# A second split level for the second MLP product of a DiT block, with inner weight sets made in the first half

## The chip, the cores and the metric

The kernel runs on one core of a Trainium2 chip. The metric is the device time of one execution in microseconds. All data is fp32. The engines of a core are TensorE (PE, with its weight loads as PEld), VectorE (DVE), ScalarE (ACT), GpSimd (POOL) and SyncE (SP), which only issues transfers.

## The reference

One DiT block on x of 2 x 2048 tokens with 576 channels: adaptive layer norm, attention with 16 heads, a projection with gated residual, a second adaptive layer norm and an MLP of width 2304 with a gated residual. The part that the change touches is the MLP:

```python
x = x + g_msa[:, None, :] * o
xn2 = _ln(x, 1e-06)
xn2 = xn2 * (1 + sc_mlp[:, None, :]) + sh_mlp[:, None, :]
h = jax.nn.gelu(xn2 @ w1 + b1, approximate=False)   # 576 -> 2304
m = h @ w2 + b2                                     # 2304 -> 576
x = x + g_mlp[:, None, :] * m
```

## The kernel before

Tokens are worked in 8 blocks (NB) of 512 (BLK). P is 128, PAIR 256, C 576, HALF 288. The width of 2304 is 18 groups (NF) of 128, of which HF = 9 make a half, and MH is 1152. Everything ahead of the MLP's two products is untouched, but for how w1 is brought in.

**The first half** makes gelu(xn2 @ w1 + b1) in 72 jobs, 9 for each token block. A job is one product of 512 tokens with 2 x 128 columns of w1, split once in the manner of Strassen and Winograd: seven products of 256 x 256 pieces in place of eight. `whole_part` is 28 matmul instructions of 256 columns (L1977), `last_part` 8 more in single-pass f32r for the last 64 rows (L1991). The weights and their sums lie in `wb` (seven sets). Two PSUM tiles, the sides, are used in turn, so a side is written again two jobs later. Then `gelu_stored`: ACT copies one product out of PSUM (L2003), DVE combines the seven in four operations that read PSUM (L2004 to L2011), ACT applies gelu to two 128x512 pieces (L2015) and SP stores each to `gelus` in DRAM (L2016, 256 KB). The four results lie in a ring of two `cs` tiles.

Between the jobs `ahead` prepares the next block's tokens, tile by tile of 128, one tile for two jobs: POOL loads a tile (L1026), DVE makes its statistics and normalizes it (L277, L279, L283, L288; ACT gives the root, L281, with a table load), DVE transposes 32x32 squares (L1042), POOL stores them to DRAM in four pieces, `turned` (L1047), and loads them back turned, whole chunks into `xnt` (L1055) and the last 64 rows twice into `parts` (L1057); ACT modulates both (L1064, L393, L394), POOL forms a difference (L395). `token_sums` adds the block's outer token sums on DVE.

**The second half** multiplies with w2 and adds the residual: 16 groups q of 256 tokens, each again split once, seven products of 128 tokens x 1152 x 288, nine matmuls of 288 columns each, which the program issues as two instructions: 2016 of L2137. Four weight quarters and three sums lie in `ws`, made in the first half. The token sums `as` are five DVE operations of 128x1152 for each q (L2115); DVE combines and applies gate and residual (L2141 to L2174), POOL adds the gated bias to the residual rows (L2120) and issues the output (L2175). `hidden` is loaded by SP, three slots of 2.3 MB. The first two products of a group use `hidden` as it is.

**What sets the order.** DVE's order is the one in which the code is written (`manual_schedule`). For PE, ACT, POOL and SP the scheduler places instructions, each engine then works its list strictly in order. A DMA stands in the queue of the engine that issues it and waits there.

The lines:

Of the kernel before, what the change touches and what calls it, by code (L numbers as in the profile page):

```python
# [8 lines left out]
F32 = mybir.dt.float32  # L9
# [22 lines left out]
def dit_block(  # L32
# [724 lines left out]
    def block_of_small():  # L757
# [1111 lines left out]
        gelus = [dram.tile([NPART, P, NF, PAIR], F32, name=f"gelu{n}") for n in range(NB)]  # L1869
# [11 lines left out]
        wb = mw.tile([P, 7, 2, MH], F32, name="wb")  # L1881
# [4 lines left out]
        for i, (k, f) in enumerate(((0, 0), (0, 1), (1, 0), (1, 1))):  # L1886
            nc.scalar.dma_start(
                out=wb[:, i],
                in_=w1[k * PAIR : (k + 1) * PAIR, f * MH : (f + 1) * MH].rearrange("(k p) f -> p k f", p=P),
            )  # L1890
        nc.scalar.dma_start(out=last_rows, in_=w1[512:576, :].rearrange("p (a f) -> p a f", a=2))
        for j in range(TPB + 1):
# [10 lines left out]
            lambda: nc.vector.tensor_tensor(wb[:, 4], wb[:, 1], wb[:, 0], ALU.subtract),  # L1903
            lambda: nc.vector.tensor_tensor(wb[:, 1], wb[:, 3], wb[:, 1], ALU.subtract),
            lambda: nc.vector.tensor_tensor(wb[:, 5], wb[:, 3], wb[:, 4], ALU.subtract),
            lambda: nc.vector.tensor_tensor(wb[:, 6], wb[:, 5], wb[:, 2], ALU.subtract),
# [23 lines left out]

        close_xs = token_tiles(3)
        m2, close_m2 = opened("m2", side="right")
        ws = {m: m2.tile([P, HF, HALF], F32, name=f"ws{m}") for m in (2, 5, 3, 4, 6, 7)}
        hidden = [m2.tile([P, NF, PAIR], F32, name="hidden0")]
# [3 lines left out]
        css = [m1.tile([P, 5, PAIR], F32, name=f"cs{i}") for i in range(2)]  # L1938
# [20 lines left out]
        def whole_part(n, f, side):  # L1959
# [15 lines left out]
            for m in (2, 4, 1, 5, 6, 7, 3) if n == f == 0 else (2, 4, 5, 6, 7, 3, 1):  # L1975
                for k in range(2):
                    nc.tensor.matmul(  # L1977
                        out_m[m],
                        wb[:, slot[m], k, f * P : (f + 1) * P],
                        moving[m](k),  # L1980
                        start=k == 0 and m in (1, 2, 5, 6),
                        stop=k == 1 and m == 1,
                    )
# [15 lines left out]
        def gelu_stored(n, f, side):  # L1999
            cs = css[side]  # L2000
# [11 lines left out]
            for i in range(2):  # L2012
                part = cs[:, 2 * i : 2 * i + 2, :]
                g = i * HF + f
                nc.scalar.activation(part, part, AF.Gelu, bias=b1_sb[:, g : g + 1])  # L2015
                nc.sync.dma_start(out=gelus[n][:, :, g, :].rearrange("t p c -> p t c"), in_=part)  # L2016
# [25 lines left out]
        quarters = [(2, 0, 0), (5, 1, 1), (3, 0, 1), (4, 1, 0)]  # L2042

        def quarter_loaded():
            m, k, n = quarters.pop(0)
            quarter = w2[k * HF * P : (k + 1) * HF * P, n * HALF : (n + 1) * HALF]
            nc.sync.dma_start(out=ws[m], in_=quarter.rearrange("(f p) c -> p f c", p=P))

        later_sums = [
            lambda: nc.vector.tensor_tensor(ws[6], ws[2], ws[3], ALU.add),  # L2050
            lambda: nc.vector.tensor_tensor(ws[3], ws[3], ws[5], ALU.subtract),
            lambda: nc.vector.tensor_tensor(ws[7], ws[4], ws[5], ALU.add),
            lambda: nc.vector.tensor_tensor(ws[4], ws[4], ws[2], ALU.subtract),
        ]

        def hidden_loaded(q):
            n, g = divmod(q, NPART)
            nc.sync.dma_start(out=hidden[q % len(hidden)], in_=gelus[n][g])
# [6 lines left out]
        for job in range(0, NB * HF, 2):  # L2065
# [13 lines left out]
            if job % 4 == 2 and job > 2 * HF and later_sums:  # L2079
                later_sums.pop(0)()  # L2080
            if job % 4 == 2 and quarters:
                quarter_loaded()
            if job == 4 * HF:
                hidden_loaded(0)
        stack.close()
        for close in (close_m1, close_mw, close_mx):
            close()

        close_psum = opened_psum(s=4)
        hs, close_hs = opened("hs")  # L2090
        hidden += [hs.tile([P, NF, PAIR], F32, name=f"hidden{i}") for i in (1, 2)]
        for q in (1, 2):
            hidden_loaded(q)
        ws[1] = hs.tile([P, HF, HALF], F32, name="ws1")

        def second_product(q, gate, gate_bias):

            b, t0 = divmod(q * PAIR, N)
            ht = hidden[q % len(hidden)]

            def part(t, k):
                return ht[:, k * HF : (k + 1) * HF, t * P : (t + 1) * P]

            stationary = {3: part(0, 0), 4: part(1, 1)}
            for m, x_, y_, op in (
                (2, part(1, 0), part(1, 1), ALU.add),
                (5, part(0, 0), part(0, 1), ALU.add),
                (6, part(1, 0), part(0, 0), ALU.subtract),
                (7, part(0, 1), part(1, 1), ALU.subtract),
                (1, part(0, 0), part(1, 1), ALU.add),  # L2110
            ):
                if q == 0 and m == 1:
                    nc.vector.tensor_tensor(ws[1], ws[2], ws[5], ALU.add)
                stationary[m] = hs.tile([P, HF, P], F32, name=f"as{m}")
                nc.vector.tensor_tensor(stationary[m], x_, y_, op)  # L2115
            xr = []
            for t in range(2):
                xr.append(hs.tile([P, C], F32, name="xr", bufs=2))
                nc.sync.dma_start(out=xr[t], in_=x1_dram[b, t0 + t * P : t0 + (t + 1) * P, :])
                nc.gpsimd.tensor_tensor(xr[t], xr[t], gate_bias, ALU.add)  # L2120
            last = q == NB * NPART - 1
            y = [hs.tile([P, 2, HALF], F32, name="y", bufs=3) for _ in range(2)]
            c00, c01, c10, c11 = y[0][:, 0, :], y[0][:, 1, :], y[1][:, 0, :], y[1][:, 1, :]
            ms = {}

            def half(ap, n):
                return ap[:, n * HALF : (n + 1) * HALF]

            def half_stored(t, n):
                nc.sync.dma_start(out=half(out[b, t0 + t * P : t0 + (t + 1) * P, :], n), in_=y[t][:, n, :])  # L2130

            for pair in ((3, 4), (2, 5), (6, 7), (1,)):
                ps = s_tile()
                for a, m in enumerate(pair):
                    ms[m] = ps[:, a, :HALF]
                    for f in range(HF):
                        nc.tensor.matmul(  # L2137
                            ms[m], stationary[m][:, f, :], ws[m][:, f, :], start=(f == 0), stop=(f == HF - 1)
                        )
                if pair == (3, 4):  # L2140
                    nc.vector.tensor_copy(c01, ms[3])  # L2141
                    nc.vector.tensor_copy(c10, ms[4])
                elif pair == (2, 5):
                    nc.vector.tensor_tensor(c00, c10, ms[5], ALU.subtract)
                    nc.vector.tensor_tensor(c11, c01, ms[2], ALU.subtract)
                    nc.vector.tensor_tensor(c10, c10, ms[2], ALU.add)
                    nc.vector.tensor_tensor(c01, c01, ms[5], ALU.add)
                elif pair == (6, 7):
                    nc.vector.tensor_tensor(c11, c11, ms[6], ALU.add)
                    nc.vector.tensor_tensor(c00, c00, ms[7], ALU.add)  # L2150

                if last and len(pair) == 2 and pair != (3, 4):
                    for t in range(2):
                        n = 1 - t if pair == (2, 5) else t
                        part = y[t][:, n, :]
                        nc.vector.tensor_tensor(part, part, half(gate, n), ALU.mult)
                        nc.vector.tensor_tensor(part, part, half(xr[t], n), ALU.add)
                        if pair == (2, 5):
                            half_stored(t, n)
            if last:  # L2160
                for t in range(2):
                    product = half(xr[t], t)
                    nc.vector.tensor_tensor(product, ms[1], half(gate, t), ALU.mult)  # L2163
                    nc.vector.tensor_tensor(y[t][:, t, :], y[t][:, t, :], product, ALU.add)  # L2164
                    half_stored(t, t)
                return
            if q + 3 < NB * NPART:
                hidden_loaded(q + 3)
            nc.vector.tensor_tensor(c00, ms[1], c00, ALU.add)
            nc.vector.tensor_tensor(c11, ms[1], c11, ALU.add)  # L2170
            for t in range(2):
                rows = y[t].rearrange("p a f -> p (a f)")
# [11 lines left out]
        for close in (close_psum, close_hs, close_m2, close_xs):  # L2184
            close()
# [39 lines left out]
```

## Time and profile before

| | |
|---|---|
| median of 3 executions | 3128.21 us (3128.03 to 3128.23) |
| the profiled execution | 3129.05 us, span 3127.3 us |
| first half, 72 jobs | one job is 7.00 us |
| second half | from 2631.70 us, 488.89 us on PE |
| granted TensorE clock | 1.00 |
| matmul instructions in the second half | 2016 |

How to read it: times in the trace are counted from the span's start. A group's row gives line, engine, operation, output<-input and shapes, the count, then busy microseconds and mean nanoseconds of one, then the idle time of the engine ahead of it and what ended that. A pipelined matmul's mean is its latency and not the distance to the next. A row of a DMA group ends with the median time from issue to landing. A row of windows gives a stretch and for PE, PEld, DVE, ACT and POOL the busy share with the count of instructions, then the granted clock, the DMA engines' busy share and GB/s. A row of one line gives the least, median and greatest duration.

### The profile page before, as it was taken

The page shows a single profiled execution, that of the slowest core. Times are in us where ns is not written, and L with a number is a line of the kernel's source. Part 1 is how long each engine was busy: PE and PEld are TensorE (multiplying, and loading weights), DVE is VectorE, ACT ScalarE, POOL GpSimd, SP SyncE. Part 2 cuts the span into 40 slices and gives each one's busy share as a digit, 9 for nine tenths or more (in the row PEclk, how much of TensorE's full clock was granted, in tenths as well). Part 3 has the DMA queues.
Part 4 walks back from the last instruction along what each step waited for, and adds up shares of the span by engine and source line. Part 5 has one row for each costly group of instructions (what it writes and reads, how often), then busy time and mean ns, then how long its engine had stood idle before and what let it go on. Part 6 is the DMA issues. An engine that isn't in the chain of part 4 may idle for free. (4 is left out here: it accounts for less than half of the span.)

```text
span 3127.3 us, 47006 instructions
## 1 busy us (share of the span) xinstructions
PE 3100.6 (99%) x17511; PEld 1849.1 (59%) x17511; DVE 1568.5 (50%) x2287; ACT 1477.3 (47%) x2853; POOL 712.6 (23%) x1005
## 2 busy tenths in 40 slices
PE   8999999999999999999999999999999999999999
PEld 5883333333333788533333333368888888777777
DVE  6773444444443556444444444355565554545454
ACT  2336666766667033466666666624565541000000
POOL 4650100132321355200011111013333320112111
PEclk9999999999999999999999999999999999999999
DMA  5773332233332654411122221146554434333331
GB/s 147 189 144 85 101 92 58 68 95 98 92 107 60 211 112 78 88 44 44 36 61 79 80 65 60 54 168 195 160 141 133 125 110 165 106 121 126 109 106 39
DMA packets 294838, 324.65 MB, mean 104 GB/s; under 512 B 168904, under 2 KB 225160, under 8 KB 292488
## 3 DMA queue, kind: packets, MB, share of 16 engines
q1 hardware_dynamic: 246464, 198.32, 21.9%
q0 software_dynamic: 46960, 117.92, 14.5%
q10 hardware_dynamic: 1176, 5.31, 0.5%
q8 instruction: 141, 2.31, 0.3%
q14 instruction: 97, 0.79, 0.1%
HBM read 200.50 MB, written 110.43 MB: 99 GB/s over the span
## 5 line engine op out<-in xcount | busy, mean ns | idle before, releaser
L1540 ACT ACTIVATE pt<-b 128x512 f32<-128x512 f32 x2048 | 1057.4, 608 | 482.0 <-PE b L1549 267.6
L1549 PE MATMUL b<-pt,vt 128*64 128x512 f32 x4096 | 935.0, 598 | 1.8 <-ACT pt L1540 1.8
L1549 PEld LDWEIGHTS b<-pt,vt 128*64 128x64 f32 x4096 | 271.8, 136 | 583.9 <-issue 437.7
L1536 PE MATMUL b<-qm,km 32*128 32x512 f32 x4096 | 563.8, 613 | 0.0
L1601 DVE TENSOR_TENSOR ot<-b,ot 128x512 f32<-128x512 f32 x192 | 132.8, 692 | 588.7 <-PE b L1549 588.7
L1536 PE MATMUL b<-qe,ke 16*128 16x512 f32 x2048 | 420.1, 791 | 0.0
L2137 PE MATMUL s<-ws,as 128*128 128x288 f32 x1440 | 351.8, 406 | 0.0
L1536 PEld LDWEIGHTS b<-qm,km 32*128 32x128 f32 x4096 | 190.6, 184 | 271.2 <-ACT pt L1540 211.1
L2137 PEld LDWEIGHTS s<-ws,as 128*128 128x128 f32 x1440 | 273.6, 190 | 75.6
L1143 PE MATMUL s<-wq,xnt 128*128 128x288 f32 x864 | 226.9, 406 | 2.5 <-ACT xnt L400 2.1
L1568 DVE RECIPROCAL den<-den 128x512 f32<-128x512 f32 x64 | 213.6, 3337 | 11.8 <-DMA den<-den_dram 11.8
L1977 PE MATMUL m<-xnt,wb 128*128 128x256 f32 x864 | 210.6, 379 | 2.6 <-DVE cs L2011 1.6
L1977 PE MATMUL m<-s,wb 128*128 128x256 f32 x864 | 210.0, 379 | 0.0
L1599 DVE COPY ot<-b 128x512 f32<-128x512 f32 x64 | 44.3, 692 | 273.3 <-PE b L1549 273.3
L1143 PEld LDWEIGHTS s<-wq,xnt 128*128 128x128 f32 x864 | 157.9, 190 | 38.3 <-ACT xnt L400 1.6
L1977 PEld LDWEIGHTS m<-s,wb 128*128 128x128 f32 x864 | 164.2, 190 | 22.3
L1536 PEld LDWEIGHTS b<-qe,ke 16*128 16x128 f32 x2048 | 106.7, 184 | 114.0 <-issue 113.3
L1977 PEld LDWEIGHTS m<-xnt,wb 128*128 128x128 f32 x864 | 158.8, 190 | 22.8 <-DVE cs L2011 2.5
L1047 POOL DMA_DIRECT2D turned<-squares x160 | 107.8, 681 | 197.6 <-DVE squares L1042 189.5
L2015 ACT ACTIVATE cs<-cs,b_sb 128x512 f32<-128x512 f32 x144 | 98.9, 719 | 113.0 <-DVE cs L2010 89.3
L1064 ACT ACTIVATE xnt<-xnt,mod 128x128 f32<-128x128 f32 x244 | 100.4, 481 | 98.4 <-DMA weight_sums<-sums_kept 51.3
L2137 PE MATMUL s<-ws,hidden 128*128 128x288 f32 x576 | 142.3, 406 | 0.0
(257 smaller groups left out, 3273.3 us busy)
## 6 DMA issues: line engine op xcount, KB each, us to landing
gelu<-cs SPq DMA_DIRECT2D x144, 256.0 KB
hidden<-gelu SPq DMA_DIRECT2D x16, 2304.0 KB
spare<-in_x_dram POOLq DMA_DIRECT2D x64, 288.0 KB, 3.1
x_dram<-spare POOLq DMA_DIRECT2D x64, 288.0 KB, 2.5
qm<-qk SPq DMA_DIRECT2D x256, 64.0 KB
den<-den_dram SPq DMA_DIRECT2D x128, 128.0 KB
xnt<-turned POOLq DMA_DIRECT2D x56, 256.0 KB, 4.0
turned<-squares POOLq DMA_DIRECT2D x160, 72.0 KB, 2.6
```

What stands on the lines that cost most here:

```text
L1047: queue.dma_start(out=by_square[g], in_=squares[g * SQ : (g + 1) * SQ, :].rearrange("p (k j) -> p k j", j=SQ))
L1064: nc.scalar.activation(part, part, AF.Identity, **affine(which, k, b))
L1143: nc.tensor.matmul(out_a, full[:, k, :], wq[:, k, f], start=k == 0, stop=False)
L1536: nc.tensor.matmul(ps, k[r, keys], q[r, :], start=first, stop=not first)
L1540: nc.scalar.activation(pt[:, h, :], banks[2 * c + h], AF.Exp, scale=SCALE)
L1549: nc.tensor.matmul(acc[64 * h : 64 * h + 64, :], vt[:, v0 : v0 + 64], pt[:, h, :], start=pt is pts[0][0], stop=pt is pts[-1][0],)
L1568: nc.vector.reciprocal(den, den)
L1599: nc.vector.tensor_copy(ot, acc)
L1601: nc.vector.tensor_tensor(ot, acc, ot, ALU.add)
L1977: nc.tensor.matmul(out_m[m], wb[:, slot[m], k, f * P : (f + 1) * P], moving[m](k), start=k == 0 and m in (1, 2, 5, 6), stop=k == 1 and m == 1,
L2015: nc.scalar.activation(part, part, AF.Gelu, bias=b1_sb[:, g : g + 1])
L2137: nc.tensor.matmul(ms[m], stationary[m][:, f, :], ws[m][:, f, :], start=(f == 0), stop=(f == HF - 1))
```

## The change

The second product is split twice. A block of 512 tokens x 2304 is split into four outer quadrants of 256 x 1152, giving seven outer products m (in the order 1, 2, 6, 5, 7, 4, 3); each of them is split again into pieces of 128 tokens x 512 and 144 columns, seven inner products of four matmuls, and a tail of 128 rows of the 1152 that the split leaves over, four matmuls. In all 56 block products with 32 matmuls of 144 columns, each again two instructions.

The parts:
- The 7 x 7 weight sets, 31 x 144 columns for each outer product, are made by DVE in the first half out of w2, two steps behind each pair of jobs (`weights_made`), in place of `quarter_loaded` and `later_sums`: 37 operations. SP stores them in 31 pieces to `w_kept` and loads them back, 2.28 MB for each outer product. `wb` is laid out anew, by f first, so that its early part can take weights once a job has used it.
- The outer token sums are made in `gelu_stored` on POOL, four of 128x256 for each job; the seven are stored in one transfer of 917 KB to `operands`. `cs` has seven pieces and a ring of three.
- The inner token sums, four of 128x512 for each block product, are made on POOL for even products and on DVE for odd ones, in two buffers, one product ahead (`sums_made`).
- DVE combines a block product in five operations out of PSUM, after a copy by ACT (`combined_blocks`), then the outer ones in SBUF, 128x576. An operand of 1.18 MB is loaded for each product, three slots.

The core of the diff:

```diff
-        gelus = [dram.tile([NPART, P, NF, PAIR], F32, name=f"gelu{n}") for n in range(NB)]
+        QUARTER = HALF // 2
+        WSIZE = 31 * QUARTER
+        operands = [dram.tile([7, P, HF, PAIR], F32, name=f"operands{n}") for n in range(NB)]
...
-            nc.scalar.dma_start(
-                out=wb[:, i],
-                in_=w1[k * PAIR : (k + 1) * PAIR, f * MH : (f + 1) * MH].rearrange("(k p) f -> p k f", p=P),
-            )
+            for j in range(2):
+                rows = slice(k * PAIR + j * P, k * PAIR + (j + 1) * P)
+                nc.scalar.dma_start(
+                    out=wb[:, :, i, j, :],
+                    in_=w1[rows, f * MH : (f + 1) * MH].rearrange("p (f c) -> p f c", c=P),
+                )
...
-        css = [m1.tile([P, 5, PAIR], F32, name=f"cs{i}") for i in range(2)]
+        css = [m1.tile([P, 7, PAIR], F32, name=f"cs{i}") for i in range(3)]
...
                 nc.scalar.activation(part, part, AF.Gelu, bias=b1_sb[:, g : g + 1])
-                nc.sync.dma_start(out=gelus[n][:, :, g, :].rearrange("t p c -> p t c"), in_=part)
+            tt = nc.gpsimd.tensor_tensor
+            tt(cs[:, 5, :], cs[:, 1, :], cs[:, 3, :], ALU.add)
+            tt(cs[:, 6, :], cs[:, 5, :], cs[:, 0, :], ALU.subtract)
+            tt(cs[:, 1, :], cs[:, 0, :], cs[:, 1, :], ALU.subtract)
+            tt(cs[:, 4, :], cs[:, 2, :], cs[:, 6, :], ALU.subtract)
+            nc.sync.dma_start(out=operands[n][:, :, f, :].rearrange("i p c -> p i c"), in_=cs)
...
+            steps = [
+                load,
+                lambda: None,
+                lambda: tt(all_[:, 4], side, all_[:, 0], ALU.subtract),
...
+                lambda: tt(more[:, :, 3], y22, y12, ALU.subtract),
...
-            if job % 4 == 2 and quarters:
-                quarter_loaded()
+            for _ in range(2):
+                if job >= 2 and making_weights:
+                    making_weights.pop(0)()
...
+        def sums_made(i):
+
+            x_ = operand[i % 3]
+            a11, a12, a21, a22 = (
+                x_[:, FULL * k : FULL * (k + 1), t * P : (t + 1) * P] for t in range(2) for k in range(2)
+            )
+            sums = hs.tile([P, 4, FULL, P], F32, name="sums", bufs=2)
+            tt = (nc.vector if i % 2 else nc.gpsimd).tensor_tensor
+            tt(sums[:, 0], a21, a22, ALU.add)
+            tt(sums[:, 1], sums[:, 0], a11, ALU.subtract)
+            tt(sums[:, 2], a11, a21, ALU.subtract)
+            tt(sums[:, 3], a12, sums[:, 1], ALU.subtract)
+            return {1: a11, 2: a12, 3: sums[:, 3], 4: a22, 5: sums[:, 0], 6: sums[:, 1], 7: sums[:, 2]}
...
+            for group in ((1,), (2, 6), (5, 7), (4, 3)):
...
+                        nc.tensor.matmul(
+                            out_m[m],
+                            stationary[m][:, c, :],
+                            w[:, FULL * (m - 1) + c, :],
...
+            tt(left, outs[2, 6], both(one), ALU.add)
+            tt(right, outs[5, 7], both(left[:, 1]), ALU.add)
+            tt(left[:, 1], right[:, 1], out_m[4], ALU.subtract)
+            tt(right[:, 1], right[:, 1], out_m[5], ALU.add)
+            tt(right[:, 0], right[:, 0], out_m[3], ALU.add)
...
+            now = stationary
+            if i + 1 < len(products):
+                stationary = sums_made(i + 1)
+            out_m, outs = multiplied(i, now)
+            operand_loaded(i + 3)
```

Where instructions stand now. First POOL in the first half, at the token tiles 46 and 47 (numbers behind names are those of the program; L2022 to L2025 are the four outer sums of a job, L1055 and L1057 the loads of a tile, L1047 its stores, L1026 the load of a tile to come). Before:

```order
L1055 DMA xnt_17613<-turned_19177 128x4x128
L1057 DMA parts_17614<-turned_19177 64x128 x2
L1047 DMA turned_19268<-squares 32x18x32 x4
L395 TENSOR_TENSOR parts_17614<-tail_17615,parts_17614 128x128
L1026 DMA xt_17958<-x_dram 128x576
L1055 DMA xnt_17613<-turned_19268 128x4x128
```

And with the change, the sums of jobs 25 and 26 around the same steps:

```order
L2022 TENSOR_TENSOR cs_17978<-cs_17978 128x256
L2023 TENSOR_TENSOR cs_17978<-cs_17978 128x256
L2024 TENSOR_TENSOR cs_17978<-cs_17978 128x256
L2025 TENSOR_TENSOR cs_17978<-cs_17978 128x256
L1055 DMA xnt_17617<-turned_19188 128x4x128
L1057 DMA parts_17618<-turned_19188 64x128 x2
L1047 DMA turned_19293<-squares 32x18x32 x4
L2022 TENSOR_TENSOR cs_17979<-cs_17979 128x256
L395 TENSOR_TENSOR parts_17618<-tail_17619,parts_17618 128x128
L2023 TENSOR_TENSOR cs_17979<-cs_17979 128x256
```

The tile's loads stand behind a job's four sums, and the first of the sums, L2022, waits for that job's gelu.

ACT at the same place (L393 and L394 modulate the parts, L2008 was L2003, the copy, and L2020 was L2015, the gelu). Before:

```order
L2003 COPY cs_17975<-one 128x256
L281 ACT_TABLE_LOAD
L281 ACTIVATE std<-mv,eps_65 128x1
L1064 ACTIVATE xnt_17613<-xnt_17613,mod 128x128 x4
L393 ACTIVATE parts_17614<-parts_17614,mod 128x128
L394 ACTIVATE tail_17615<-parts_17614,mod 128x128
L2015 ACT_TABLE_LOAD
L2015 ACTIVATE cs_17975<-cs_17975,b_sb 128x512 x2
```

And with the change:

```order
L2008 COPY cs_17979<-one 128x256
L281 ACT_TABLE_LOAD
L281 ACTIVATE std<-mv,eps_65 128x1
L1064 ACTIVATE xnt_17617<-xnt_17617,mod 128x128 x4
L393 ACTIVATE parts_17618<-parts_17618,mod 128x128
L394 ACTIVATE tail_17619<-parts_17618,mod 128x128
L2020 ACT_TABLE_LOAD
L2020 ACTIVATE cs_17979<-cs_17979,b_sb 128x512 x2
```

ACT's order is the same: a tile's modulation stands between a job's copy and its gelu, and waits for the loads that POOL issues.

Last, POOL at the end of the first half (L2183 to L2186 are inner sums of the first block product; cs_17979 is that of the last job). Before, the second half begins on POOL with residual rows:

```order
L395 TENSOR_TENSOR parts_17617<-tail_17618,parts_17617 128x128
L2120 TENSOR_TENSOR xr<-xr,gate_21030 128x576 x2
L2175 DMA out_dram<-y 128x576 x2
```

With the change:

```order
L2022 TENSOR_TENSOR cs_17979<-cs_17979 128x256
L2023 TENSOR_TENSOR cs_17979<-cs_17979 128x256
L2024 TENSOR_TENSOR cs_17979<-cs_17979 128x256
L2025 TENSOR_TENSOR cs_17979<-cs_17979 128x256
L2183 TENSOR_TENSOR sums<-operand_17965 128x512
L2185 TENSOR_TENSOR sums<-operand_17965 128x512
L2184 TENSOR_TENSOR sums<-sums,operand_17965 128x512
L2186 TENSOR_TENSOR sums<-operand_17965,sums 128x512
```

The inner sums of the first block product stand behind the outer sums of the last job, and the one that m = 6 needs, L2184, is the third.

More of the change, by code (lines that the diff above doesn't have):

```diff
@@ L2092, in block_of_small @@
[L2092 to L2138, printed above, removed]
-                        )
[L2140 to L2172, printed above, removed]
-                nc.vector.tensor_tensor(rows, rows, gate, ALU.mult)
-                nc.vector.tensor_tensor(rows, rows, xr[t], ALU.add)
-                nc.gpsimd.dma_start(out=out[b, t0 + t * P : t0 + (t + 1) * P, :], in_=rows)
@@ L2177, in block_of_small @@
[L2177 to L2182 removed]
+        operand += [
+            spots[:, 3 * WSIZE : 3 * WSIZE + HF * PAIR].rearrange("p (f c) -> p f c", f=HF),
+            hs.tile([P, HF, PAIR], F32, name="operand2"),
+        ]
@@ L2183, in block_of_small @@
         in_order.__exit__(None, None, None)
-        for close in (close_psum, close_hs, close_m2, close_xs):
+        for close in (close_psum, close_hs, close_mb, close_m2):
             close()
```

202 lines of the change are left out of this document (165 added, 37 removed).

## The prediction

> **What bounds the kernel now.** I read the page first, then the chain that ended last.
>
> ```profile
> span 3127.3 us, 47006 instructions
> PE 3100.6 (99%) x17511; PEld 1849.1 (59%) x17511; DVE 1568.5 (50%) x2287; ACT 1477.3 (47%) x2853; POOL 712.6 (23%) x1005
> PEclk9999999999999999999999999999999999999999
> ```
>
> PE is busy for 99% of the span at the full granted clock and every other engine for half of it or less. So a saving has to come out of PE's own time, and whatever makes PE wait is a loss in full. The chain of waits from 2600 us on shows PE's two last stages, one behind the other with no gap:
>
> ```profile
> 2624.70 5.18 PE m L1977 x24
> 2629.88 0.86 PE one L1977 x4
> 2630.74 0.95 PE m L1991 x8
> 2631.70 488.89 PE s L2137 x2016
> ...
> 3121.97 0.46 DVE y L2164
> ```
>
> The first three rows are one job of the first MLP half: 7.00 us, 72 times. The fourth is the whole second product. Between its end, 3120.59, and the span's end lie 6.7 us. The groups of PE and its weight loads in that stretch:
>
> ```profile
> L2137 PE MATMUL s<-ws,as 128*128 128x288 f32 x1440 | 351.8, 406 | 0.0
> L1977 PE MATMUL m<-xnt,wb 128*128 128x256 f32 x840 | 204.7, 379 | 1.7 <-DVE cs L2011 1.6
> L2137 PEld LDWEIGHTS s<-ws,as 128*128 128x128 f32 x1440 | 273.6, 190 | 75.6
> ```
>
> The means of 406 and 379 ns are latencies of overlapping instructions, not what one costs; the cost is the chain's time by its count. PE waits for DVE 1.6 us in a whole half: in the first half the other engines keep up, but each has only 7 us a job.
>
> **The change part by part.** All sums are against the profiled run, 3129.05 us, 1.75 above its span; the median shown is 3128.21, so 0.84 comes off at the end.
>
> *Second product on PE.* Removed are 2016 matmuls of 288 columns, added 56 products x 32 x 2 = 3584 of 144 columns, each with a weight load as before. Cost of one now: 488.89/2016 = 242.5 ns at 288 columns; 5.18/24 = 215.8 ns at 256. The line through both has 0.834 ns a column and gives 122.4 ns at 144, so 438.5 us: **-50**. This is an estimate below the columns that the rows show. Lower bound: eight L1991 matmuls, each with its 128x128 load, take 0.95 us, 118.8 ns each, and there the load and not the columns may set the pace; at that the term is -63. Upper bound: the densest long stretch of load and matmul pairs in the trace,
>
> ```profile
> 900.00:1000.00 100.00, 100.00 (x668) 37.20 (x668) 40.11 (x50) 69.19 (x135) 22.36 (x34) 1.00 0.32 86
> ```
>
> 668 pairs in 100 us, 149.7 ns each, though these matmuls have 512 columns; at that it would be +48. I take 122.4, since the two f32 rows with the same 128x128 load are nearest. The Trainium skill's TensorE: Matmul & The Clock Gate (Back-to-back issue gap) gives a sustained roofline of about 131 ns for 512 columns and 81 for 128, and N/2.4 + 2.5 ns for a matmul alone. The 256-column f32 rows here cost 215.8 ns, what the formula gives for 512 and far from 131, so the trace sides with the formula; by the roofline the term would be some -120.
>
> *Start of the second half.* In before the first two products need no sums. After, POOL has to make the last job's four outer sums and then the inner sums of the first block product, and PE has only its blocks m=1 and m=2 (9 x 2 x 0.122 = 2.2 us) before m=6, which needs the third POOL operation. The rows:
>
> ```profile
> 2631.79 0.69 DVE L2004 TENSOR_TENSOR cs<-m,cs 128x512 f32<-128x512 f32 x1 [4.41 <-PE m L1991]
> 2633.70 0.69 DVE L2011 TENSOR_TENSOR cs<-cs,m 128x512 f32<-128x512 f32 x1
> 2633.74 1.40 ACT L2015 ACTIVATE cs<-cs,b_sb 128x512 f32<-128x512 f32 x2 [2.54 <-DVE cs L2010]
> L1267 POOL TENSOR_TENSOR more<-xnt 128x256 f32<-128x256 f32 x7 | 5.1, 728 | 0.0
> L1661 POOL TENSOR_TENSOR spare<-spare 128x576 f32<-128x576 f32 x32 | 45.7, 1429 | 0.9 <-DMA spare<-in_x_dram 0.4
> ```
>
> Gelu ends 3.45 us after PE's last first-half matmul (T = 2631.69). Four sums of 0.73 bring POOL to T+6.4; an inner sum of 512 lies between 728 and 1429 ns, 1.29 by the line, three to T+10.2. Less 2.2 that is a gap of 8. If DVE's sums of the next product hold POOL's up (below) it is 11. I take **+9**, range 7 to 12.
>
> *End.* After the last matmul come three DVE operations of 144 columns, three of 576 and a POOL-issued store, where before had four short ones.
>
> ```profile
> L2174 DVE TENSOR_TENSOR y<-y,xr 128x576 f32<-128x576 f32 x30 | 22.8, 758 | 3.5 <-DVE y L2173 0.5
> L2157 DVE TENSOR_TENSOR y<-y,xr 128x288 f32<-128x288 f32 x4 | 1.8, 458 | 0.3
> out_dram<-y POOLq DMA_DIRECT2D x30, 288.0 KB, 4.1
> ```
>
> By the line through 458 and 758, 144 columns take 0.31: 3 x 0.31 + 3 x 0.76 + 0.55 to issue + 4.1 = 7.9 against 6.7, **+1**.
>
> *First half, where the new work goes.* POOL gets four 128x256 sums per job, 5.8 us per pair of jobs. Beside them it has the token tile of the block to come, one per pair:
>
> ```profile
> L1047 POOL DMA_DIRECT2D turned<-squares x108 | 72.8, 681 | 159.6 <-DVE squares L1042 155.4 <-DVE cs L2004 2.3 <-issue 1.9
> L1057 POOL DMA_DIRECT2D parts<-turned x54 | 29.1, 544 | 2.4 <-issue 2.4
> L1055 POOL DMA_DIRECT2D xnt<-turned x27 | 20.4, 757 | 76.2 <-DMA turned<-squares 41.4 <-PE one L1977 23.7 <-PE m L1991 11.2
> L395 POOL TENSOR_TENSOR parts<-tail,parts 128x128 fp32r<-128x128 f32 x28 | 13.0, 466 | 40.5 <-ACT tail L394 40.1
> L1026 POOL DMA_DIRECT2D xt<-x_dram x18 | 10.4, 577 | 0.0
> parts<-turned POOLq DMA_DIRECT2D x54, 32.0 KB, 3.3
> ```
>
> 4 x 0.68 + 2 x 0.54 + 0.76 + 0.47 + 0.58 = 5.6. Together 11.4 of 14 us: it fits as a sum. But POOL takes its work in order, and the outer sums wait for gelu; the tile's loads stand behind them, and ACT has the tile's modulation standing ahead of the next job's copy and gelu:
>
> ```profile
> L2015 ACT ACTIVATE cs<-cs,b_sb 128x512 f32<-128x512 f32 x142 | 97.5, 719 | 110.5 <-DVE cs L2010 86.8 <-issue 23.4
> L2003 ACT COPY cs<-one 128x256 f32<-128x256 f32 x71 | 25.9, 365 | 72.1 <-PE one L1977 71.9
> L281 ACT ACT_TABLE_LOAD x26 | 33.4, 1283 | 0.5
> ...
> 2414.19 0.48 ACT L393 ACTIVATE parts<-parts,mod 128x128 fp32r<-128x128 f32 x1
> 2414.58 0.48 ACT L394 ACTIVATE tail<-parts,mod 128x128 f32<-128x128 f32 x1
> ```
>
> That closes a ring which before does not have. From the end of one job's gelu: four sums and two load issues 4.0, landing 3.3, the two modulations 0.9, a table load 1.3, the next job's gelu 1.4, together 10.9 where PE's pace is 7. From there to the gelu after it are copy, DVE's part and gelu, 0.4 + 1.95 + 1.4 = 3.7: the pair takes 14.6 us against 14. In the order of the change 15 of the 27 tiles have both, the loads behind an odd job's sums and the modulation between copy and gelu, in runs of 3, 4, 2 and 4 and two alone. At the others the ring has a job more to close in. PE is covered for a while: a job's PSUM side is written again two jobs later, so DVE's 2.6 us for it (2631.79 to 2634.39 above) may start 4.4 late. At 0.6 a tile, a run of four would stay inside. But the landing is from a quieter half:
>
> ```profile
> 2400.00:2500.00 100.00, 100.00 (x517) 89.64 (x517) 53.54 (x99) 57.62 (x103) 34.82 (x57) 1.00 0.47 130
> ```
>
> The DMA engines are 0.47 busy at 130 GB/s. The change stores 917 KB per job where it was 512, +58 GB/s, and 31 weight stores of 516 KB in 448 us, +36; at the row's share per byte that is 0.81. If the 3.3 us grows like that, by 0.7, it is 5.6; if not at all, 3.3.
>
> DVE makes the weight sets in the same time: 16 operations of 576 columns, 17 of 1008, 4 of 288. With 758 ns and the 1352 below for 1152 columns, 1008 take 1.20: 34 us in 32 pairs. DVE has room for that. But:
>
> ```profile
> L2115 DVE TENSOR_TENSOR as<-hidden x80: 1345/1352/2564, 2634.3 to 3101.4; 128x1152 f32<-128x1152 f32 x80
> L2120 POOL TENSOR_TENSOR xr<-xr,gate x32: 1401/2068/2538, 2651.8 to 3098.8; 128x576 f32<-128x576 f32 x32
> ```
>
> Where these two meet, DVE's goes from 1352 to 2564 ns and POOL's from 1401 to 2538: one waits for most of the other. Both read two operands from SBUF. So DVE's weight work holds up POOL's ring, about 1.1 us a pair if every operation meets one. I take landings 1.5 longer and half the meetings: 14.6 + 1.5 + 0.55 is 2.7 late a tile, and what goes beyond the cover of 4.4 is 3.7 + 6.4 + 1.0 + 6.4 in the four runs, 17.5; with some for the mixed places between them **+20**. Bounds: 0 as worked out from today's landing, and 15 x (0.6 + 2.3 + 1.1 + 0.6 for one more table load in two) = 69 with no cover. The Trainium skill's SBUF — State Buffer (Who interferes with whom) has one port pair that a GpSimd operation and a DVE operation with two SBUF inputs lock for a whole instruction; the trace agrees (+1212 and +1137 ns), and if every weight operation stopped POOL within the ring, the term would be some 34 us more.
>
> *Smaller.* The first weights arrive in rows of 512 bytes: 0 to 3 us, **+1**; the 31 weight stores and 72 stores of 917 KB go on SP, which waits in order for POOL, with three cs slots where DVE had two: in the ring already.
>
> *Second half, in the running.* A block product lasts 64 x 0.122 = 7.8 us. Its inner sums start when the product before last has let go of their buffer and are due 7.8 + 2.2 = 10 us later. DVE needs some 2.8, POOL 5.2, and 9.3 + 2.5 for a residual sum if each meets DVE. So only POOL's products that carry a residual sum can be late, at most 16 x 1.8 = 29; **+4**, range 0 to 29. Loads of 1.18 MB per 7.8 us are 151 GB/s, below what moved elsewhere.
>
> **Sum:** -50 + 9 + 1 + 20 + 1 + 4 = -15; 3129.05 - 15 - 0.84 = **3113**.
>
> **The rivals.** *The cover holds* (B): landings stay near 3.3 us, lateness is given back between the runs, and 0 to 8 us of the 20 remain. For it: PE waited 1.6 us in the half before, and POOL idles 160 us before L1047. 3129.05 - 0.84 - 35 is 3093: it gives 3093 to 3101, and 3089 without the second half's 4. *The ring paces the first half* (C, slower): landings grow, each tile that closes the ring is 2.7 to 4.6 us late, and the tiles between give nothing back: 40 to 69 us, and -35 for everything else gives 3133 to 3162. It decides from 35/15 = 2.3 us a tile not covered. For it speaks the DMA share worked out above, against it that 12 of 27 tiles and the block borders are slack. *PE doesn't reach 122 ns* (D): the load, 118.8 ns at best here, then has 4 ns of cover where it had 124. The other terms are +35, so the gain is gone at (488.9 - 35)/3584 = 126.6 ns a pair; at 131 the time is 3144. Against it: both f32 rows lie on one line, and the L1991 rows run at 118.8 for eight in a row. That the change does not do what it says I leave out: the count of matmuls and columns is fixed in the code.
>
> **How the numbers follow.** Main case 0.49 (3103 to 3130), B 0.20, C 0.18, D 0.13. Range 3088 to 3150: it leaves out 0.07 of C, 0.03 of D, 0.02 of B and some 0.06 for costs beyond their bounds. A measurement of this kernel tells about 0.2%, 6.3 us, from no change. Below 3122.0 lie 0.44 of the main case, all of B and 0.02 of the rest: 0.66. Above 3134.5 lie 0.15 of C and 0.05 of D: 0.20. Between: 0.14.
>
> **What would show it.** PE's chain in the second product: 122 to 123 ns a matmul is right, 127 or more is D. A gap of 8 to 11 us before m=6 of the first product, ending with POOL. The first half's chain: jobs of 7.0 us with PE waiting for DVE's cs operations, DVE for ACT's copy, that behind L393 which waits for the parts' load; if PE stays at 7.00 throughout, B. DVE's 1008-column operations lengthened to twice their shortest show the meetings. The prediction is wrong if the first half's stretch is under 8 or over 40 us, or a pair costs over 126.6 ns.

## The result and the profile after

The changed kernel takes 3164.36 us (median of 4, 3162.72 to 3166.24) against 3128.22 (3128.03 to 3128.85): a ratio of 1.0115, 95% interval 1.0098 to 1.0133. It is 36 us slower, where 3113 was forecast, and beyond the range's upper end of 3150. The profiled execution took 3162.72 us, 33.7 more than before's.

The page, first part, with PE's slices of the span (40 equal ones; a digit is the busy share in tenths, 9 is 90% or more):

```profile
span 3160.9 us, 51170 instructions
PE 3075.0 (97%) x19079; PEld 1917.0 (61%) x19079; DVE 1677.7 (53%) x2521; ACT 1493.4 (47%) x2909; POOL 1081.0 (34%) x1407
PE   8999999999999999999999999999888999899998
```

PE's busy time fell by 26 us, but three slices in the first MLP half, the 29th to the 31st, and the 35th, where the second half begins, are no longer full. Where the halves begin and end is read from the rows of the matmul lines (count, least, median and greatest duration, first and last start). Of before, then of the changed kernel:

```profile
L1977 PE MATMUL m<-xnt,wb x864: 377/379/484, 2124.7 to 2628.6; 128*128 128x256 f32 x173
L2137 PE MATMUL s<-ws,hidden x576: 404/406/406, 2631.5 to 3098.3; 128*128 128x288 f32 x192
```

```profile
L1982 PE MATMUL m<-xnt,wb x864: 377/379/796, 2122.9 to 2698.7; 128*128 128x256 f32 x173
L2201 PE MATMUL b<-w_first,operand x384: 283/286/286, 2701.6 to 3119.3; 128*128 128x144 f32 x192
```

The first half went from 506.8 to 578.7 us, **+72**. The second, to its last matmul's end, went from 489.0 to 450.8, **-38**. The tail behind it grew from 6.7 to 8.5, **+1.9**, and the first half began 1.8 earlier. Together 33.8, which is the whole difference. The first half as one stretch, of before, then of the changed kernel:

```profile
2124.70:2631.50 506.80, 505.07 (x2592) 451.85 (x2593) 275.24 (x486) 261.66 (x457) 149.60 (x244) 1.00 0.48 139
2122.90:2701.60 578.70, 526.97 (x2592) 460.43 (x2593) 323.74 (x519) 262.51 (x457) 359.84 (x528) 0.98 0.72 216
```

Here the numbers behind the length are busy microseconds. PE stood idle 51.7 us of the changed half, where before it stood idle 1.7, and the DMA engines were 0.72 busy instead of 0.48. What PE waited for in the changed kernel, in total, times and longest:

```profile
PE one L1982 <- ACT cs L2008: 30.5, 18, 4.2
PE m L1982 <- DVE cs L2016: 21.2, 23, 4.5
PE b L2201 <- POOL sums L2184: 8.4, 1, 8.4
```

The same view of the first half, for ACT and POOL. The first row is of before, the others of the changed kernel:

```profile
ACT xnt L1064 <- DMA xnt<-turned: 13.3, 6, 6.6
ACT xnt L1064 <- DMA xnt<-turned: 117.7, 27, 7.3
ACT parts L393 <- DMA parts<-turned: 17.2, 12, 3.8
...
POOL cs L2022 <- ACT cs L2020: 134.0, 46, 6.1
```

This is the ring: POOL waits for ACT's gelu, ACT waits for transfers that POOL issued behind its sums. All 27 tiles now wait for `xnt`, where before 6 did. One turn of it on ACT, in order of time:

```profile
2458.64 1.33 ACT L2020 ACTIVATE cs<-cs,b_sb 128x512 f32<-128x512 f32 x2 [2.37 <-DVE cs L2015]
...
2467.03 1.65 ACT L1064 ACTIVATE xnt<-xnt,mod 128x128 f32<-128x128 f32 x4 [5.18 <-DMA xnt<-turned]
2469.71 0.49 ACT L393 ACTIVATE parts<-parts,mod 128x128 fp32r<-128x128 f32 x1 [1.04 <-DMA parts<-turned]
2470.11 0.48 ACT L394 ACTIVATE tail<-parts,mod 128x128 f32<-128x128 f32 x1
2470.61 1.28 ACT L2020 ACT_TABLE_LOAD   x1
2471.90 1.33 ACT L2020 ACTIVATE cs<-cs,b_sb 128x512 f32<-128x512 f32 x2
```

and on POOL:

```profile
2460.05 0.73 POOL L2022 TENSOR_TENSOR cs<-cs 128x256 f32<-128x256 f32 x1 [0.59 <-ACT cs L2020]
2461.53 0.76 POOL L1055 DMA_DIRECT2D xnt<-turned  x1 [0.74 <-DMA turned<-squares]
...
2464.57 1.08 POOL L1057 DMA_DIRECT2D parts<-turned  x2
...
2473.31 0.73 POOL L2022 TENSOR_TENSOR cs<-cs 128x256 f32<-128x256 f32 x1 [2.19 <-ACT cs L2020]
```

From the gelu's end at 2459.97 to that of the next job at 2473.23 are 13.3 us, where PE's pace is 7. It is a usual turn: over the 27 jobs with a modulation the median from gelu's end to gelu's end is 13.0 us (8.8 before), 26 of them lie between 11.3 and 16.5, and over the jobs without a modulation the median is 3.7. DVE had its input for the second gelu ready by 2465.3, as its row shows:

```profile
2464.89 0.42 DVE L2015 TENSOR_TENSOR cs<-cs,m 128x256 f32<-128x256 f32 x1
```

But that gelu stood behind the modulation, that behind `xnt`, and the load of `xnt` behind the first sum and the stores of the squares.

A slower clock comes on top. A job's start in the chain, after a wait and two jobs later:

```profile
2337.38 8.14 PE m L1982 x24
...
2354.32 5.18 PE m L1982 x24
```

24 matmuls take 3.0 us more after a wait of 4.5. The rows of windows give the granted clock (third last):

```profile
2337.00:2346.00 9.00, 8.62 (x27) 7.11 (x28) 7.38 (x10) 2.72 (x5) 8.56 (x12) 0.67 0.63 157
2300.00:2400.00 100.00, 87.30 (x421) 75.98 (x420) 57.26 (x89) 46.94 (x81) 65.46 (x97) 0.95 0.69 199
```

The waits booked above are PE's idle time of 51.7 us and account for 50 of the 72, as before had 1.7. The other 22 lie in PE's busy time, 527.0 us against 505.1 for the same 2592 matmuls. A mean clock of 0.98 over 578.7 us makes about 12 of them, by estimate; the rest I have not separated.

The landings in the first half (median us, last number), before:

```profile
turned<-squares POOLq DMA_DIRECT2D x108, 72.0 KB, 2.6
xnt<-turned POOLq DMA_DIRECT2D x27, 256.0 KB, 3.9
```

and after:

```profile
turned<-squares POOLq DMA_DIRECT2D x108, 72.0 KB, 4.7
xnt<-turned POOLq DMA_DIRECT2D x27, 256.0 KB, 5.7
parts<-turned POOLq DMA_DIRECT2D x54, 32.0 KB, 5.0
```

### The profile page after: what moved, and what is told of

Same layout as the page of the kernel before. It is cut to its first block, busy times and chain, and to the rows that moved or that the text cites. A ratio compares the mean times of both kernels' runs of the same rounds, so it can differ in the third digit from the quotient of the medians.

```text
span 3160.9 us, 51170 instructions
## 1 busy us (share of the span) xinstructions
PE 3075.0 (97%) x19079; PEld 1917.0 (61%) x19079; DVE 1677.7 (53%) x2521; ACT 1493.4 (47%) x2909; POOL 1081.0 (34%) x1407
## 4 chain that ended last, share of the span: by engine, by line
PE 81%; DMA 6%; POOL 4%; issue 3%; DVE 3%; ACT 3%; SPq 0%; POOLq 0%; DVEq 0%; ACTq 0%
PE b L1549 29%; PE b L1536 20%; PE b L2201 12%; PE s L1143 6%; PE s L1229 5%; PE m L1982 3%; DMA xnt<-turned 2%; PE s L411 2%; PE b L2210 2%; DMA parts<-turned 1%; DMA turned<-squares 1%; PE s L1145 1%; ACT cs L2020 1%; PE s L1235 1%; POOL cs L2023 1%
## 5 line engine op out<-in xcount | busy, mean ns | idle before, releaser
L1982 PE MATMUL m<-xnt,wb 128*128 128x256 f32 x864 | 217.0, 388 | 22.1 <-DVE cs L2016 21.2
L2218 ACT COPY one<-b 128x144 f32<-128x144 f32 x56 | 15.6, 278 | 425.1 <-PE b L2201 409.9
L1658 POOL DMA_DIRECT2D spare<-in_x_dram x32 | 17.7, 554 | 442.7 <-DVE met L796 442.7
L2020 ACT ACTIVATE cs<-cs,b_sb 128x512 f32<-128x512 f32 x144 | 99.4, 719 | 106.0 <-DVE cs L2015 105.7
L2009 DVE TENSOR_TENSOR cs<-m,cs 128x512 f32<-128x512 f32 x72 | 49.2, 683 | 185.9 <-ACT cs L2008 145.7
L817 POOL DMA_DIRECT2D km<-qk x56 | 28.1, 502 | 322.8 <-PE b L1536 321.3
```

The source lines that it names most:

```text
L1982: nc.tensor.matmul(out_m[m], wb[:, f, slot[m], k, :], moving[m](k), start=k == 0 and m in (1, 2, 5, 6), stop=k == 1 and m == 1,)
```

## Experiments

Three theories of the 72 us. **T**: the ring's transfers land later because SP's stores fill the DMA engines. **S**: POOL's and ACT's order closes the ring, at any landing. **P**: DVE's weight operations block POOL. Each kernel ran once beside before on the same chip (3128.1 to 3129.4), the last two four times. The halves are of one profiled execution each. Kernels whose first half is written alike give its spread: changed and x12 differ by 0.9 us, and x9, x11, x14 and x15 lie between 510.0 and 513.5.

| kernel | us | first half | second half |
|---|---|---|---|
| before | 3128.2 | 506.8 | 489.0 |
| changed | 3164.4 | 578.7 | 450.8 |
| e1_no_weights | 3146.8 | 561.4 | 450.4 |
| e2_no_weight_stores | 3158.5 | 571.5 | 450.5 |
| e3_small_stores | 3132.6 | 546.4 | 451.3 |
| e4_sums_dve | 3127.5 | 527.0 | 465.5 |
| x5_look | 3153.6 | 569.8 | 449.6 |
| x10_order | 3190.4 | 605.9 | 450.2 |
| x8_manual | 3117.1 | 525.0 | 458.5 |
| x9_manual_nolate | 3101.3 | 512.7 | 451.1 |
| x12_swap | 3167.6 | 579.6 | 452.5 |
| x11_last_weights | 3097.1 | 510.3 | 451.7 |
| x14_second_order | 3089.3 | 513.5 | 442.3 |
| x15_second_order_pool | 3091.2 | 510.0 | 445.2 |

### Taking the traffic and the weight work away

e1, without the weight sets:

```diff
-    making_weights = [do for c in (0, 1, 2, 3, 2 * FULL) for do in weights_made(c)] + [firsts_loaded]
+    making_weights = [lambda: None] * 62 + [firsts_loaded]
...
-            nc.sync.dma_start(out=dst, in_=w_kept[m - 1])
+            kept = w2.rearrange("k c -> (k c)")[0 : P * WSIZE].rearrange("(p f) -> p f", f=WSIZE)
+            nc.sync.dma_start(out=dst, in_=kept)
```

> Leaves out the making of the 49 weight sets (loads of w2 pieces, 37 DVE operations, 31 stores); the second half loads raw w2 instead. Theory T (the transfers of the ring land later because SP's stores fill the DMA engines): the first half, 72 us longer than before with the change, loses 15 to 30 of it, since 16 MB of small-packet stores go. Theory P (DVE's weight operations hold POOL up at their shared port): 30 or more go. Theory S (POOL's place in the ring alone, at any landing): under 10.

e2, without their stores alone:

```diff
             def stored(j, src):
-                nc.sync.dma_start(
-                    out=w_kept[:, :, j * QUARTER : (j + 1) * QUARTER].rearrange("i p f -> p i f"), in_=src
-                )
+                pass
```

> Keeps the 37 DVE operations and the loads of w2 pieces, leaves out the 31 weight stores; the second half loads raw w2. Theory T: nearly all that e1 gains, 12 us or more, and the median landing of turned falls from 4.7 us. Theory P: within 5 us of the changed kernel. Theory S: within 5.

e3, as many bytes stored per job as before the change:

```diff
-            nc.sync.dma_start(out=operands[n][:, :, f, :].rearrange("i p c -> p i c"), in_=cs)
+            nc.sync.dma_start(out=operands[n][0:4, :, f, :].rearrange("i p c -> p i c"), in_=cs[:, 0:4, :])
...
-        at_operand = {1: 0, 2: 2, 3: 4, 4: 3, 5: 5, 6: 6, 7: 1}
+        at_operand = {1: 0, 2: 2, 3: 0, 4: 3, 5: 1, 6: 2, 7: 1}
```

> The order on every engine is that of the changed kernel; each job stores four of the seven outer operands (512 KB in place of 917, as many bytes as before), and the second half uses those four. Theory T: 20 to 40 us of the 72 go, landings of turned and xnt near 3.5 and 4.5 us. Theory P and theory S: under 5.

e3 is the clean one: POOL's order is the changed kernel's row for row, and 32 us of the 72 go. Its landings:

```profile
turned<-squares POOLq DMA_DIRECT2D x108, 72.0 KB, 2.9
xnt<-turned POOLq DMA_DIRECT2D x27, 256.0 KB, 4.4
```

So late landings cost about 32 us, and 40 us of stretch remain with landings near before's. S had expected under 5 here, T up to 40: each holds a part. e1 wins back 17 us, as T expected; S had under 10 and P 30 or more. e2 wins back 7, less than T's 12 and little more than the 5 that S and P had, and `turned` lands in 4.2 us there, for 4.7. In e2 POOL's and ACT's order in the first half is the changed kernel's too, so about 7 us is what the weight stores cost by this one run. In e1 the scheduler placed some of POOL's and ACT's instructions elsewhere, so e1 does not price the weight work alone, and what DVE's weight operations cost the ring (P) is not settled by the difference of 10. P as the main cause falls with e1: without any weight work 55 of the 72 us are still there.

### Taking POOL out of the ring

e4 makes the outer sums on DVE, one job late:

```diff
-            tt = nc.gpsimd.tensor_tensor
-            tt(cs[:, 5, :], cs[:, 1, :], cs[:, 3, :], ALU.add)
...
+            late.append((n, f, cs))
+            if len(late) > 1:
+                outer_sums()
+
+        def outer_sums():
+            n, f, cs = late.pop(0)
+            tt = nc.vector.tensor_tensor
+            tt(cs[:, 5, :], cs[:, 1, :], cs[:, 3, :], ALU.add)
...
```

> Nothing left out: the four outer sums of a job are made by DVE one job later, behind the next job's cs operations, so POOL's queue waits for no gelu. Theory S: 50 us or more of the 72 go, though landings stay long. Theory T: 20 to 50 go, since loads are issued earlier but still land late. Theory P: 30 or more go, since POOL has only one short sum a tile left to collide; DVE is then some 85% busy in the first half.

52 of the 72 us go, as S expected and just above what T gave; P's "30 or more" fits as well, so e4 alone does not part S from P. `xnt` still lands in 5.3 us and `parts` in 4.7. `turned` lands in 2.6, as it did before, though the DMA engines are busier than in the changed kernel (0.78 of the half against 0.72), so their share alone does not set this landing. The second half gives 15 back, since DVE's backlog now stands ahead of the first inner sums:

```profile
PE b L2210 <- DVE sums L2193: 12.5, 1, 12.5
PE b L2210 <- DMA wb<-operands: 7.3, 1, 7.3
```

### Order and look-ahead, apart and together

The sums stay on POOL. x5 gives the tiles more time and leaves the order to the scheduler; x10 writes POOL's and ACT's order out and leaves the tiles' jobs; x9 does both, and x8 also makes the sums one job late, still on POOL, with a list like e4's. x8 and x9 have the inner sums of even products on DVE, which touches the second half alone.

```diff
# x5, x8, x9
...
-            for what, todo in at(turn=-2, read=0, modulate=1, load=-5):
+            for what, todo in at(turn=-3, read=0, modulate=2, load=-6):
# x8, x9, x10
+        in_turn = tc.manual_schedule(
+            engines={mybir.EngineType.DVE, mybir.EngineType.Pool, mybir.EngineType.Activation}
+        )
+        in_turn.__enter__()
         for job in range(0, NB * HF, 2):
...
# x8, x9, x12
-            tt = (nc.vector if i % 2 else nc.gpsimd).tensor_tensor
+            tt = (nc.gpsimd if i % 2 else nc.vector).tensor_tensor
```

Of x5:

> Nothing left out. Each token tile is begun one job earlier (stores and load) and modulated one job later, which gives each landing 7 us more; sums and stores as in the changed kernel; the scheduler places POOL, ACT and SP anew. Theory T and theory S both: the first half loses 30 us or more of its 72 us of stretch if the ring opens. A theory that blames the load of POOL or DVE as such (their busy time, not the waiting): under 10.

Of x8:

> Nothing left out. Tiles begun a job earlier and modulated a job later, the outer sums written one job late, POOL and ACT in written order in the first half, and the first inner sums on DVE instead of POOL (odd products on POOL). If the stretch is a ring of waits, though DMA, POOL and DVE have the same work: first half within 15 us of before's 507, so 3090 to 3110 in all. If the engines' load or the DMA engines' share themselves set the pace: still over 540. The gap before the third block of the first product falls from 8.7 to 2 or 3 us.

Of x9:

> As x8, but the outer sums at their old place, right behind their job's gelu. If the sums' place ahead of the tile's loads matters even with a job more for each landing: 10 us or more above x8. If only the number of jobs between load and modulation matters: within 5 us of it.

Of x10:

> Nothing left out. The changed kernel with POOL and ACT in written order in the first half and nothing else: tiles begun and modulated at the old jobs, inner sums as in the change. If the places that the scheduler chose make the ring: first half under 525 us, and this stands within 15 us of x9's 513. If the job more of look-ahead is what opened it: 540 or more, as long as x5 or the changed kernel.

| first half, us | tiles at the old jobs | a job more on each side |
|---|---|---|
| scheduler's order | 578.7 | 569.8 |
| written order | 605.9 | 512.7 |

Neither does it alone. x5 was to win 30 us by S and T and won 9, which by itself fits a theory of the engines' load (under 10). But the scheduler put the modulations ahead of the gelus again, and ACT still waited for `xnt`, 107.6 us. x10 was to be near x9 if the scheduler's places made the ring, and at 540 or more if the look-ahead opened it. It is at 605.9, 27 us worse than the change, and ACT waits 124.6 us for `xnt`: in written order every modulation stands ahead of its job's copy, and its loads were issued only a job earlier. Together order and look-ahead open the ring. In x9 the waits of PE in the first half shrink to 6 us, though the landings are longer than in the changed kernel:

```profile
turned<-squares POOLq DMA_DIRECT2D x108, 72.0 KB, 5.5
xnt<-turned POOLq DMA_DIRECT2D x27, 256.0 KB, 6.2
parts<-turned POOLq DMA_DIRECT2D x54, 32.0 KB, 5.6
```

```profile
2250.00:2350.00 100.00, 100.00 (x515) 89.57 (x514) 67.42 (x113) 57.26 (x99) 80.22 (x115) 1.00 0.82 243
```

The second block is 100 us of the same half: POOL 80% busy, DMA engines 82%, all the weight operations in place, and PE full at clock 1.00. No engine's load set the pace. What did is the closed ring (S), and T's 32 us are the price of landings inside it: with the ring open, longer ones cost at most the 6 us by which x9's half still exceeds that of before. ACT reads here

```profile
2448.53 1.64 ACT L1064 ACTIVATE xnt<-xnt,mod 128x128 f32<-128x128 f32 x4
2450.07 0.48 ACT L393 ACTIVATE parts<-parts,mod 128x128 fp32r<-128x128 f32 x1
```

with no wait ahead of the modulation. x8 missed its range by a little: 525.0 where within 15 us of 507 was expected, and 3117 in all for 3090 to 3110. Its gap ahead of m = 6, counted from one matmul's start to the next, fell from the change's 8.7 to 2.2 us as expected, but two others of 5.7 and 7.0 us came in the second half. x9 was expected level with x8 or at least 10 us above it; it is 12 below in the first half: with late sums the store of a `cs` tile is late too, and ACT's copy waits for the tile to come free,

```profile
ACT cs L2008 <- DMA operands<-cs: 29.3, 12, 6.9
```

### The start of the second half

Of x12:

> Nothing left out. The changed kernel with DVE making the inner sums of even products and POOL those of odd ones, the order else left to the scheduler. The first half stays at 570 to 580. The gap before m = 6 of the first product falls from 8.7 to 2 to 3 us, as DVE is free 3 us after PE's last first-half matmul while POOL has four sums to make; if other waits take its place, the second half stays near 451.

The gap ahead of m = 6 fell from 8.7 to 2.2 us as expected, and the second half did not gain: 452.5, as the expectation allowed. Three other gaps came, 0.7, 1.6 and 4.4 us long, 27 to 40 us into it. x11, x14 and x15 are x9 with more. x11 and x14 looked for their cause: x11 was to move the last weight set (2.28 MB) behind the first operands, x14 fixes SP's order as well and loads each residual row ahead of its product.

```diff
# x11, x14, x15
-        weights_loaded(3, w_last)
...
             operand_loaded(i + 3)
+            if i == 1:
+                weights_loaded(3, w_last)
# x14, x15
+        in_turn = tc.manual_schedule(engines={mybir.EngineType.DVE, mybir.EngineType.SP})
+        in_turn.__enter__()
         for i in (1, 2):
             operand_loaded(i)
...
+            xr = residual_rows(n, *quadrant, gate_bias) if quadrant else None
             out_m, outs = multiplied(i, now)
```

x15 has POOL in that list too.

Of x11:

> Nothing left out. x9 with the last weight set (2.28 MB, first used by the seventh product) loaded after the second product instead of ahead of the first operands. If the gaps 26 to 39 us into the second half come from operand loads behind that transfer: they go, 5 to 8 us less, second half 443 to 446. If they come from the inner sums' own pace on DVE and POOL: 451 as in x9.

Of x14:

> Nothing left out. x9 with SP too in written order in the second half, so that the last weight set really goes behind the operands of the first five products, and each residual row is loaded ahead of its product. If the gaps 26 to 39 us into the second half come from operands behind that transfer: second half 441 to 446, some 3092 in all. If the inner sums' own pace makes them: 450 as in x9.

Of x15:

> As x14, with POOL in written order in the second half as well, so an output's issue, which waits for DVE, can hold up the next inner sums. If POOL's place matters: 3 to 10 us above x14; if there is room: within 2 us of it.

x11 moved nothing: the scheduler put the load back ahead of the fourth operand, and the gaps stayed. Its DVE, behind that,

```profile
2651.76 0.69 DVE L2188 TENSOR_TENSOR sums<-operand 128x512 f32<-128x512 f32 x1 [5.99 <-DMA operand<-operands]
...
2667.01 1.80 DVE L2251 TENSOR_TENSOR r<-r,xr 128x576 f32<-128x576 f32 x1 [9.14 <-POOL xr L2243]
```

waited for an operand, and 9 us in order for a residual row while the next sums stood behind it. x14 has 442.3 us in the second half, as expected, and one later gap of 0.9. So the places of the transfers on SP made the gaps; x14 moved two of them at once, the weight set's and the residual rows', and which of the two counted is not separated. x15 is 3 us longer there in its profiled execution, with three small gaps more, but in all it is 1.9 us above x14 (medians 3091.18 and 3089.32, and their intervals overlap), so whether POOL's place matters stays open.

x14 takes 3089.32 us (median of 4, 3087.59 to 3090.49), a ratio of 0.9873 to before, 95% interval 0.9857 to 0.9890. It is the change's arithmetic with another order, and beats both kernels.

## Why the prediction was wrong

**The matmuls: right.** -50 at 122.4 ns. A block product in the changed kernel's chain:

```profile
2935.09 2.94 PE b L2201 x24
...
2942.93 2.94 PE b L2201 x24
```

2.94/24 = 122.5 ns, and 7.84 us from one product to the next. The line through 256 and 288 columns held down to 144, and rival D is out.

**The start of the second half: right in mechanism, a little small.** +9 forecast; 8.4 us of waiting for L2184, the third POOL operation, and 3.0 us of slower matmuls behind it. PE's rows around it:

```profile
2703.60 0.41 PE L2210 MATMUL b<-w_first,operand 128*128 128x144 f32 x2
2712.44 6.07 PE L2201 MATMUL b<-w_first,sums 128*128 128x144 f32 x24 [8.43 <-POOL sums L2184]
2718.35 0.41 PE L2210 MATMUL b<-w_first,operand 128*128 128x144 f32 x2
```

The 24 matmuls behind the gap take 5.91 us, 246 ns each, twice the usual: 3.0 us that no term had. The Trainium skill's TensorE: Matmul & The Clock Gate (Part 1: The HAM clock gate) has the clock halved after an idle window of about 3.4 us and full again after a busy one as long. The trace agrees with the half; here it holds for 5.9 us of matmuls, longer than one such window.

**The tail: right.** +1 forecast, +1.9 measured. **The first weights:** +1 forecast, with no row behind it; the half began 1.8 us earlier. No run shows a cost of the 512-byte rows: among the kernels with the change the half began between 2122.9 and 2126.6 us, with nothing different ahead of it. **Second half in the running:** +4 forecast, under 1 measured (450.8 less 439.0, the gap and the slow matmuls).

**The first half: this step failed.** I had +20 and it was +72. The ring was named, and rival C, "the ring paces the first half", is what happened, at 3164, just above its 3133 to 3162. C too counted 15 tiles, at up to 4.6 us each, so that its upper end lies near is chance. What failed in the working:

- "15 of the 27 tiles" close the ring, and the others have "a job more to close in"; and the cover of 4.4 us was taken off in each of four runs. The waits' row has 27 modulations waiting for `xnt`, that is every tile, and 26 of the 27 turns last 11.3 us or more. Hardly any tile was slack, and no run of tiles got its cover back. By the measured medians a pair of jobs is 13.0 + 3.7 = 16.7 us where PE's pace is 14, so 2.7 late, and 27 times that is 73, the whole stretch. The prediction had the 2.7 too, for fifteen tiles, less the covers.
- The ring's path. The first turn, "together 10.9 where PE's pace is 7", went through `parts` alone; with 1.5 for the landing and 0.55 for meetings with DVE it is 13.0, the measured median. The size is right, but in part by luck: `xnt` and `turned` were in no term of it, and the path goes through them. `xnt` stands behind a sum too, waits for the stores of the squares and takes 5.7 us to land; ACT waited 117.7 us for `xnt` and 17.2 for `parts`. How many of the twelve tiles that were held to be slack are closed by this path alone is not separated.
- A wait was priced at its length. After a longer one PE runs at half the clock for a time, as in the 8.14 us above.

The landing was nearly right, +1.5 us forecast and 1.7 measured for `parts`, from the DMA share. What it is worth in all was not: e3 says 32 us, more than the whole term of 20, since every tile pays for it. Rival B's argument, that PE waited 1.6 us before and POOL idled 160 us, fails too, as idle time is no room in a closed ring: in the changed kernel POOL still waits 134.0 us for the gelu while PE waits 52, and x9's POOL is busier and PE waits 6.

## What to carry over

When work is put on an in-order engine, draw every transfer that this engine issues behind it up to where its landing is next waited for, and back to the new work: a closed ring sets a pace of its own, whatever the busy shares. Here look-ahead and order had to be changed together: look-ahead alone won 9 us, and order alone lost 27. A cover of a few microseconds is used up once when every tile is late.

## What the runs showed that I had not expected

DVE's operation with one input, L288, is also held up by POOL. Least, median and greatest of it in the changed kernel:

```profile
L288 DVE TENSOR_SCALAR xt<-xt,mv,rstd x28: 578/590/2826, 22.9 to 2590.8; 128x576 f32<-128x576 f32 x28
```

The longest of them, and what POOL did meanwhile:

```profile
2478.78 2.83 DVE L288 TENSOR_SCALAR xt<-xt,mv,rstd 128x576 f32<-128x576 f32 x1
2479.19 0.74 POOL L2023 TENSOR_TENSOR cs<-cs 128x256 f32<-128x256 f32 x1
2479.88 0.73 POOL L2024 TENSOR_TENSOR cs<-cs 128x256 f32<-128x256 f32 x1
2480.56 0.72 POOL L2025 TENSOR_TENSOR cs<-cs 128x256 f32<-128x256 f32 x1
```

It ends behind the third of POOL's sums. Before, the greatest of these 28 was 689. I had counted only operations with two inputs from SBUF. The Trainium skill's SBUF — State Buffer (Who interferes with whom) counts tensor_scalar among those that can take the shared port pair; the trace agrees with 2826 against 578 ns.
